# Layer 0's FFN: four constant products a block taken from VectorE, one to ScalarE and three to GpSimd

## The chip, the cores and the metric

The kernel runs on one core of a Trainium2 chip. The core has a matrix engine (TensorE, PE in the profile; its weight loads are PEld), a vector engine (VectorE, DVE), an activation engine (ScalarE, ACT), GpSimd (POOL) and SyncE (SP), which issues most transfers. Each engine works through its own queue in order and waits on semaphores for the others. The metric is the device time of one execution in microseconds. The matrix engine's clock can be throttled; the profile shows the granted share of full speed.

## What is computed

Two transformer layers over x of shape (2, 1024, 256), 2048 tokens in all. Each layer normalises x and adds an attention and an FFN of the same normalised input:

```python
x = L0_attn_x
xn = _layernorm(x, axis=-1)
x = x + _L0_attn_ref(xn, ...) + _L0_ffn_ref(xn, L0_ffn_w_gating, L0_ffn_w_linear)
xn = _layernorm(x, axis=-1)
x = x + _L1_attn_ref(xn, ...) + _L1_ffn_ref(xn, L1_ffn_w_gate_up, L1_ffn_w_proj)
```

The change lies in layer 0's FFN, with inputs rounded to an 8-bit float and results in bfloat16:

```python
def _qdot(x, w, out_dtype=BF16):
    return jnp.dot(x.astype(E4M3), w.astype(E4M3), preferred_element_type=out_dtype)
ff_gate = _qdot(x, w_gating[0])
gate_value = jax.nn.gelu(ff_gate)
ff1 = _qdot(x, w_gating[1])
activations = gate_value * ff1
outputs = _qdot(activations, w_linear)
```

gelu is the tanh form: with g the gate, 0.5 (1 + tanh(c0 (g + c1 g^3))) g, every step rounded to bfloat16. Layer 0's attention is causal, with 32 heads of 8 columns over 1024 keys, and takes an exact maximum of each row of scores before the exponentials. Layer 1's attention is over 16 heads for each token, its FFN has ternary weights.

## The kernel before

Layer 0 is one loop over slots in `attention0`. A slot is one call of `weigh` (L929): four matmuls give two score tiles of 128 keys x (4 heads x 128 queries) (L934), two exponentials on ScalarE turn them into p (L944), on the diagonal GpSimd clears what lies above it (L948), and one group later `gather` (L962) multiplies p with the values (L964). There are 288 such slots, for 16 blocks of 128 queries (`order`).

Between them, ahead by three query blocks, run the units of maxima (`max_unit`, L859): matmuls of scores into PSUM (L870, and L847 for the causal mask), and a reduction by VectorE over the keys (L882). Their tiles have three PSUM buffers. A finished block of maxima goes through L909 and L911, by DRAM, into rows of `qlast`, and its queries come by L799; the loop starts a query block only ten slots after its maxima (`LEAD`).

`one_slot` (L1134) paces three things into each slot: units of maxima by a credit, and one piece of layer 0's FFN at a time, so that 171 pieces spread over the slots. A piece is what lies between two `yield`s of `weights0` (L203, the rounding of the weights) or `ffn0` (L231). A piece is issued under `tc.issue_after(reduced.ins)`, that is, behind the last reduction given out so far. TensorE's order is that of the program text (`manual_schedule` for PE); for the other engines the framework's scheduler orders the queues.

`ffn0` works through four chunks of 512 tokens, and in each through four blocks `h2` of two hidden chunks: 16 blocks. A block makes gate and f1 for 2 x 128 hidden columns (L283), which ScalarE copies to bfloat16 tiles of 128 x 1024, `g` and `f1` (L286). Then come Square on ScalarE (L289) and the gelu chain on VectorE (L290 to L300) with Tanh on ScalarE in its middle (L295). The function `e4m3` (L182) rounds the product to the 8-bit grid in four steps (L190, L193, L195, L198) and a fifth, the check (L200), multiplies by a large constant and its inverse so that what overflows the format becomes infinite or not a number, as in the reference. The tiles `fs` (f1 and w1), `fg` (g), `fw` (w2) and `fe` have one buffer each, `act` has five. When a chunk's four `act` tiles are there and the next chunk's first block is through, `out_piece` (L240) makes the output matmuls (L243); ScalarE copies them (L252, L253) and GpSimd adds them to x (L256).

GpSimd also rounds layer 1's weights to ternary values, four steps for each of twelve pieces (L333 to L336) followed by a load (L321), and does part of preparing queries and keys (L711, L715, L750) and the residual adds of attention (L1007, L1008).

Of the kernel before, what the change touches and what calls it, by code (L numbers as in the profile page):

```python
# [11 lines left out]
BF = mybir.dt.bfloat16  # L12
I32 = mybir.dt.int32
U16 = mybir.dt.uint16
AF = mybir.ActivationFunctionType
ALU = mybir.AluOpType
# [28 lines left out]
E4_BIG = 1.109375 * 2.0**119  # L45
# [3 lines left out]
def two_layers(ctx: ExitStack, tc: tile.TileContext, a: dict, out: bass.AP):  # L49
    nc = tc.nc  # L50
# [128 lines left out]
                nc.scalar.copy(xnT[c][:, k, :], ps[k])  # L179
            yield  # L180

    def e4m3(dst, src, e, s, check):  # L182

        wide = src.dtype == F32
        as_int = I32 if wide else U16
        big = 1.5 * 2.0 ** (20 if wide else 4)
        nc.vector.tensor_scalar(  # L190
            e.bitcast(as_int), src.bitcast(as_int), 0x7F800000 if wide else 0x7F80, None, ALU.bitwise_and
        )
        nc.vector.tensor_scalar(e, e, E4_MIN, big, ALU.max, ALU.mult)  # L193
        yield
        nc.vector.tensor_tensor(s, src, e, ALU.add)  # L195
        if wide:
            yield
        nc.vector.tensor_tensor(dst, s, e, ALU.subtract)  # L198
        if check:
            nc.vector.tensor_scalar(dst, dst, E4_BIG, 1.0 / E4_BIG, ALU.mult, ALU.mult)  # L200


    def weights0(pool, scratch):  # L203

        wg = pool.tile([P, 2, 2, HID], BF, tag="wg", name="wg", bufs=1)
        wl = pool.tile([P, NHC, D], BF, tag="wl", name="wl", bufs=1)
        stage = scratch
        dst = [wg[:, g, k, :] for g in range(2) for k in range(2)]
        dst += [wl[:, 4 * h : 4 * h + 4, :].rearrange("p c d -> p (c d)") for h in range(2)]

        def load(n):
            st = stage[n % 4]
            if n < 4:

                (nc.sync if n < 1 else nc.gpsimd).dma_start(out=st, in_=a["w_gating"][n // 2, n % 2 * P : n % 2 * P + P, :])
            else:
                nc.gpsimd.dma_start(
                    out=st.rearrange("p (c d) -> p c d", d=D),
                    in_=a["w_linear"][(n - 4) * 512 : (n - 3) * 512, :].rearrange("(c p) d -> p c d", p=P),
                )  # L220

        load(0)
        yield wg, wl
        for n in range(6):
            e, s = (pool.tile([P, 1024], F32, tag=x, name=f"{x}w{n}", bufs=1) for x in ("fe", "fs"))
            yield from e4m3(dst[n], stage[n % 4], e, s, True)
            for m in range(1, 4) if n == 0 else [n + 3] if n < 3 else []:
                load(m)
            yield

    def ffn0(pool, psp, weights, add_done):  # L231

        wg, wl = weights
        acts = {}

        def e_tile(dt, name):
            t = pool.tile([P, 1024], F32, tag="fe", name=name, bufs=1)
            return t if dt == F32 else t.bitcast(BF)[:, 0:1024]

        def out_piece(n, i):  # L240
            po = psp.tile([P, D], F32, tag="t", name=f"f0o{n}_{i}")
            for hc in range(NHC):
                nc.tensor.matmul(  # L243
                    po,
                    acts[n][hc // 2][:, hc % 2 * 512 + i * P : hc % 2 * 512 + (i + 1) * P],
                    wl[:, hc, :],
                    start=(hc == 0),
                    stop=(hc == NHC - 1),
                )

            ob = pool.tile([P, 2, D], BF, tag="ob", name=f"ob{n}_{i}", bufs=1)
            nc.scalar.copy(ob[:, 0], po)  # L252
            nc.scalar.activation(ob[:, 1], po, AF.Copy, scale=0.0)  # L253
            x_i = xs[4 * n + i]
            for j in range(2):
                nc.gpsimd.tensor_tensor(x_i, x_i, ob[:, j], ALU.add)  # L256
            add_done(4 * n + i)

        order = (0, 1, 3, 2)
        for m, n in enumerate(order):  # L260
            wide = pool.tile([P, 1024], F32, tag="fs", name=f"fsx{n}", bufs=1)
            xq = pool.tile([P, 2, 512], BF, tag="xq", name=f"xq{n}", bufs=1)
            yield from e4m3(
                xq.rearrange("p k t -> p (k t)"),
                xnT[n].rearrange("p k t -> p (k t)"),
                e_tile(F32, f"fex{n}"),
                wide,
                False,
            )
            yield  # L270
            acts[n] = []
            for h2 in range(NHC // 2):
                nm = f"{n}_{h2}"
                wide = pool.tile([P, 1024], F32, tag="fs", name=f"fs{nm}", bufs=1)
                w1, f1 = (wide.bitcast(BF)[:, k * 1024 : (k + 1) * 1024] for k in range(2))
                g = pool.tile([P, 1024], BF, tag="fg", name=f"fg{nm}", bufs=1)
                w2 = pool.tile([P, 1024], BF, tag="fw", name=f"fw{nm}", bufs=1)
                for j in range(2):
                    hc = 2 * h2 + j
                    for u, to in enumerate((g, f1)):  # L280
                        ps = psp.tile([P, 512], F32, tag="t", name=f"gu{nm}_{j}{u}")
                        for k in range(2):
                            nc.tensor.matmul(  # L283
                                ps, wg[:, u, k, hc * P : (hc + 1) * P], xq[:, k, :], start=(k == 0), stop=(k == 1)
                            )
                        nc.scalar.copy(to[:, j * 512 : (j + 1) * 512], ps)  # L286
                    yield

                nc.scalar.activation(w1, g, AF.Square)  # L289
                nc.vector.tensor_mul(w1, w1, g)  # L290
                nc.vector.tensor_scalar(w1, w1, GELU_C1, None, ALU.mult)
                yield
                nc.vector.tensor_add(w1, g, w1)
                nc.vector.tensor_scalar(w1, w1, GELU_C0, None, ALU.mult)
                nc.scalar.activation(w2, w1, AF.Tanh)  # L295
                yield
                nc.vector.tensor_scalar(w2, w2, 1.0, 0.5, ALU.add, ALU.mult)
                nc.vector.tensor_mul(w2, g, w2)
                yield
                nc.vector.tensor_mul(w2, w2, f1)  # L300
                yield
                act = pool.tile([P, 1024], BF, tag="act", name=f"act{nm}", bufs=5)
                yield from e4m3(act, w2, e_tile(BF, f"fe{nm}"), w1, True)
                acts[n].append(act)
                yield
                if m and h2 == 0:
                    for i in range(4):
                        out_piece(order[m - 1], i)
                        yield
        for i in range(4):  # L310
            out_piece(order[-1], i)
            yield
# [365 lines left out]
    def attention0(w, qlast, tables):  # L678
# [11 lines left out]
        with ExitStack() as es:  # L690
# [418 lines left out]
            acc = ps_acc.tile([P, 512], F32, tag="acc", name="acc0")  # L1109
            nc.vector.memset(acc, 0.0)  # L1110
            pieces = itertools.chain(conversions, ffn0(pool, ps_t, weights, add_done))
            at = 0
            credit = share = 0.0
# [79 lines left out]
def _bf(v):  # L1193
    import ml_dtypes
    import numpy as np

    return float(np.float32(v).astype(ml_dtypes.bfloat16))
# [7 lines left out]
GELU_C0 = _bf((2.0 / PI) ** 0.5)  # L1205
GELU_C1 = _bf(0.044715)
# [77 lines left out]
```

## Time and profile before

| what | value |
|---|---|
| median of 3 runs | 1200.87 us (1200.59 to 1201.39) |
| the profiled execution's own time | 1200.35 us |
| its span, first to last instruction | 1198.6 us |
| TensorE busy in the span | 1016.8 us, 85% |
| VectorE busy | 745.6 us, 62% |
| ScalarE busy | 574.3 us, 48% |
| GpSimd busy | 335.7 us, 28% |
| mean granted clock | 0.913 |

The profile is one execution. Busy time counts the instructions of an engine; matmuls overlap and their ends are modelled. Layer 0 ends and layer 1 begins at about 780 us. The page's slices (40 equal parts of the span, tenths of busy time; a slice is 30 us) show where each engine is full:

```profile
PE   5463887897989989888989998978999999998884
DVE  6677988899688998698986888162323223323220
ACT  1112462672556757576767776731424414414421
POOL 2023233314243120412134246453312212312200
```

VectorE is nearly full up to slice 24 and a third full afterwards; TensorE is nearly full from slice 6 to the end. An idle gap on one engine is put down to what ended it: "idle before" names the instruction of another engine, or the transfer, that came last. The chain of waits goes back from the last instruction, at each step to what released it.

Rows of the VectorE chain of one block, as groups (busy us, mean ns, idle time before and what ended it):

```profile
L290 DVE TENSOR_TENSOR fs<-fs,fg 128x1024 bf16<-128x1024 bf16 x16 | 11.3, 705 | 0.0
L293 DVE TENSOR_TENSOR fs<-fg,fs 128x1024 bf16<-128x1024 bf16 x16 | 12.8, 799 | 0.0
L298 DVE TENSOR_TENSOR fw<-fg,fw 128x1024 bf16<-128x1024 bf16 x16 | 12.6, 788 | 0.3
L300 DVE TENSOR_TENSOR fw<-fw,fs 128x1024 bf16<-128x1024 bf16 x16 | 11.7, 732 | 0.0
```

### The profile page before, as it was taken

The page shows a single profiled execution, that of the slowest core. Times are in us where ns is not written, and L with a number is a line of the kernel's source. Part 1 is how long each engine was busy: PE and PEld are TensorE (multiplying, and loading weights), DVE is VectorE, ACT ScalarE, POOL GpSimd, SP SyncE. Part 2 cuts the span into 40 slices and gives each one's busy share as a digit, 9 for nine tenths or more (in the row PEclk, how much of TensorE's full clock was granted, in tenths as well). Part 3 has the DMA queues.
Part 4 walks back from the last instruction along what each step waited for, and adds up shares of the span by engine and source line. Part 5 has one row for each costly group of instructions (what it writes and reads, how often), then busy time and mean ns, then how long its engine had stood idle before and what let it go on. Part 6 is the DMA issues. An engine that isn't in the chain of part 4 may idle for free.

```text
span 1198.6 us, 18891 instructions
## 1 busy us (share of the span) xinstructions
PE 1016.8 (85%) x7228; PEld 487.4 (41%) x7228; DVE 745.6 (62%) x1416; ACT 574.3 (48%) x1006; POOL 335.7 (28%) x384
## 2 busy tenths in 40 slices
PE   5463887897989989888989998978999999998884
PEld 2231332232433222232323334234676676675663
DVE  6677988899688998698986888162323223323220
ACT  1112462672556757576767776731424414414421
POOL 2023233314243120412134246453312212312200
PEclk8676797997899989998989999999999999998985
DMA  6631001002101010101010110047111421421202
GB/s 191 157 98 37 22 5 46 11 20 60 34 17 36 3 25 19 36 1 27 2 27 3 25 27 5 2 55 114 37 28 45 76 41 42 80 41 29 45 11 53
DMA packets 79012, 48.99 MB, mean 41 GB/s; under 512 B 31721, under 2 KB 73705, under 8 KB 78921
## 3 DMA queue, kind: packets, MB, share of 16 engines
q1 hardware_dynamic: 75960, 43.58, 17.1%
q0 software_dynamic: 2960, 4.20, 1.7%
q8 instruction: 57, 0.93, 0.3%
q14 instruction: 35, 0.28, 0.1%
HBM read 33.59 MB, written 15.73 MB: 41 GB/s over the span
## 4 chain that ended last, share of the span: by engine, by line
PE 53%; DVE 25%; DMA 7%; ACT 6%; issue 4%; POOL 3%; SPq 2%; ACTq 0%; POOLq 0%; DVEq 0%
DVE mx L882 14%; PE acc L964 8%; PE f1gu L609 7%; PE s L934 7%; PE f1o L640 5%; PE m L870 4%; PE sk L519 3%; PE sq L484 3%; PE gu L283 2%; ACT p L527 2%; DMA qkv<-all 2%; PE m L847 2%; PE acc L534 2%; ACT p L944 1%; PE ao L585 1%
## 5 line engine op out<-in xcount | busy, mean ns | idle before, releaser
L882 DVE TENSOR_REDUCE mx<-m 128x1 f32<-128x512 f32 (+3 forms) x608 | 372.8, 655 | 90.0 <-PE m L870 52.1
L944 ACT ACTIVATE p<-s 128x512 f32<-128x512 f32 x576 | 306.8, 604 | 147.0 <-PE s L934 143.8
L964 PE MATMUL acc<-p,v 128*9 128x512 f32 x1152 | 172.4, 623 | 1.8 <-ACT p L944 1.2
L870 PE MATMUL m<-k,qmain 64*128 64x512 bf16 (+3 forms) x384 | 93.9, 363 | 52.9 <-DVE mx L882 36.0
L948 POOL TENSOR_SCALAR_AFFINE_SELECT p<-p 128x512 f32<-128x512 f32 x128 | 84.3, 682 | 177.2 <-ACT p L944 176.9
L609 PE MATMUL f1gu<-xnT,wgu 128*128 128x512 f32 x256 | 118.4, 606 | 1.6 <-DVE wgu L1189 1.6
L870 PE MATMUL m<-kmain,qmain 64*128 64x512 bf16 (+3 forms) x384 | 83.8, 333 | 24.3 <-DVE mx L882 22.1
L870 PEld LDWEIGHTS <-qmain 64*128 64x128 bf16 x768 | 50.2, 100 | 88.2 <-issue 63.0
L617 DVE TENSOR_TENSOR h<-f1gu,h 128x512 f32<-128x512 f32 x32 | 22.1, 692 | 99.6 <-PE f1gu L609 99.6
L621 POOL TENSOR_TENSOR sq<-h 128x512 f32<-128x512 f32 x28 | 29.1, 1039 | 189.5 <-DVE h L617 189.5
L847 PEld LDWEIGHTS <-ident_h 64*128 64x128 bf16 x832 | 45.1, 97 | 85.0 <-issue 62.2
L934 PE MATMUL s<-qlast,k 35*128 35x512 bf16 x288 | 65.4, 399 | 16.2 <-DMA qlast<-mscr 16.2
L847 PE MATMUL m<-mask_q,ident_h 64*128 64x128 bf16 (+3 forms) x832 | 75.0, 222 | 3.2 <-DVE mx L882 2.2
L934 PE MATMUL s<-qmain,k 64*128 64x512 bf16 x288 | 68.9, 400 | 8.8 <-DVE att L987 3.0
L609 PEld LDWEIGHTS f1gu<-xnT,wgu 128*128 128x128 f32 x256 | 47.8, 196 | 51.2 <-issue 48.4
L934 PE MATMUL s<-qmain,kmain 64*128 64x512 bf16 x288 | 64.1, 390 | 5.2 <-ACT p L944 2.6
L934 PEld LDWEIGHTS <-k 64*128 64x128 bf16 (+1 forms) x576 | 21.2, 96 | 114.5 <-issue 106.1
L492 DVE TENSOR_REDUCE m<-sq 128x16 f32<-128x2048 f32 x16 | 36.7, 2292 | 44.1 <-PE sq L484 42.6
L934 PE MATMUL s<-qlast,klast 35*128 35x512 bf16 x288 | 61.2, 386 | 0.0
L640 PE MATMUL f1o<-k,h 128*128 128x256 f32 x256 | 59.4, 389 | 0.0
L640 PEld LDWEIGHTS f1o<-k,h 128*128 128x128 f32 x256 | 49.4, 194 | 8.4 <-issue 1.1
L484 PE MATMUL sq<-ks,qs 24*128 24x128 f32 x512 | 34.7, 414 | 14.5 <-ACT p L527 13.7
(264 smaller groups left out, 1541.4 us busy)
## 6 DMA issues: line engine op xcount, KB each, us to landing
qmain<-qscr SPq DMA_DIRECT2D x64, 96.0 KB
qkv<-all SPq DMA_DIRECT2D x16, 384.0 KB
qscr<-ptq SPq DMA_DIRECT2D x32, 96.0 KB
x<-in_x SPq DMA_DIRECT2D x16, 128.0 KB
qmain<-qscr SPq DMA_DIRECT2D x32, 64.0 KB
qs<-qkv SPq DMA_DIRECT2D x16, 128.0 KB
ks<-qkv SPq DMA_DIRECT2D x16, 128.0 KB
vs<-qkv SPq DMA_DIRECT2D x16, 128.0 KB
```

The source lines that it names most:

```text
L484: nc.tensor.matmul(ps[:, s, r, :], columns(q, slice(S * s, S * s + HD + 8), 4 * b + r), columns(k, slice(S * s, S * s + HD + 8), 4 * b + r ...
L492: nc.vector.tensor_reduce(m, ps, AX.X, ALU.max, negate=True)
L519: nc.tensor.matmul(ps[:, s, r, :], columns(k, slice(S * s, S * s + HD + 9), 4 * b + r), columns(q, slice(S * s, S * s + HD + 9), 4 * b + r ...
L609: nc.tensor.matmul(ps[g], wgu[:, k, g * HID + hc * P : g * HID + (hc + 1) * P], xnT[n][:, k, :], start=(k == 0), stop=(k == 1),)
L640: nc.tensor.matmul(po, hs[hc // 2][:, hc % 2, i * P : (i + 1) * P], wp[:, hc, :], start=(hc == 0), stop=(hc == NHC - 1),)
L847: nc.tensor.matmul(out[e][:, :, lo:], ident_h[rows, t, :], rhs.to_broadcast([HALF, out[e].shape[1], P - lo]), start=start and t == 0, stop ...
L870: nc.tensor.matmul(sc[e][:, s * width : (s + 1) * width], qst[b, i][0][rows, p, :], kst[b][0][rows, p // 4, lo : lo + width], start=not fo ...
L882: reduced = nc.vector.tensor_reduce(mx[b, i][:, part, e, pairs[0] : pairs[0] + n], sc[e][:, : n * width].rearrange("p (s k) -> p s k", s=n ...
L934: nc.tensor.matmul(sc[e], kst[b][n][rows, u, j * P : (j + 1) * P], qst[b, i][n][rows, 4 * u : 4 * u + 4, :], start=n == 0, stop=n == 1,)
L944: nc.scalar.activation(p, sc[e], AF.Exp, scale=scale)
L948: nc.gpsimd.affine_select(out=by_head, in_=by_head, compare_op=ALU.is_ge, fill=0.0, base=0, pattern=[[0, 4], [1, P]], channel_multiplier=-1,)
L964: nc.tensor.matmul(acc[32 * s : 32 * s + HD0 + 1, :], vst[b][:, j, 4 * G + s, :], ps[s], start=(j == 0), stop=(j == i),)
```

## The change

In each of the 16 blocks of `ffn0` four products with constants leave VectorE. The product with c1 (L291), `(w2 + 1) * 0.5` (L297) and the check of `e4m3` (L200) go to GpSimd; the product with c0 (L294) becomes a Copy with a scale on ScalarE. The check of the weights in `weights0` stays on VectorE. The `yield` that stood between L298 and L300 now stands before L298, so the number of pieces is as before.

```diff
-    def e4m3(dst, src, e, s, check):
+    def e4m3(dst, src, e, s, check, checker=nc.vector):
...
         nc.vector.tensor_tensor(dst, s, e, ALU.subtract)
         if check:
-            nc.vector.tensor_scalar(dst, dst, E4_BIG, 1.0 / E4_BIG, ALU.mult, ALU.mult)
+            checker.tensor_scalar(dst, dst, E4_BIG, 1.0 / E4_BIG, ALU.mult, ALU.mult)
...
                 nc.scalar.activation(w1, g, AF.Square)
                 nc.vector.tensor_mul(w1, w1, g)
-                nc.vector.tensor_scalar(w1, w1, GELU_C1, None, ALU.mult)
+                nc.gpsimd.tensor_scalar(w1, w1, GELU_C1, None, ALU.mult)
                 yield
                 nc.vector.tensor_add(w1, g, w1)
-                nc.vector.tensor_scalar(w1, w1, GELU_C0, None, ALU.mult)
+                nc.scalar.activation(w1, w1, AF.Copy, scale=GELU_C0)
                 nc.scalar.activation(w2, w1, AF.Tanh)
                 yield
-                nc.vector.tensor_scalar(w2, w2, 1.0, 0.5, ALU.add, ALU.mult)
+                nc.gpsimd.tensor_scalar(w2, w2, 1.0, 0.5, ALU.add, ALU.mult)
+                yield
                 nc.vector.tensor_mul(w2, g, w2)
-                yield
                 nc.vector.tensor_mul(w2, w2, f1)
                 yield
                 act = pool.tile([P, 1024], BF, tag="act", name=f"act{nm}", bufs=5)
-                yield from e4m3(act, w2, e_tile(BF, f"fe{nm}"), w1, True)
+                yield from e4m3(act, w2, e_tile(BF, f"fe{nm}"), w1, True, nc.gpsimd)
```

All line numbers in this document are those of the kernel before. In the changed kernel the same lines stand one further down from L289 on, and L298 two.

## The prediction

> **What bounds the kernel now.** I read first the busy time by stage. Layer 0's FFN vector work (sixteen blocks of gelu, one per pair of hidden chunks) starts at 167 us and ends at 731 us, so the stage is 175 to 735 us. The columns are length, then busy time and count of TensorE, its weight loads, VectorE, ScalarE and GpSimd, the granted clock, DMA share and GB/s.
>
> ```profile
> 175.00:735.00 560.00, 492.99 (x3649) 166.17 (x3651) 478.27 (x904) 351.74 (x675) 171.86 (x201) 0.94 0.10 23
> 735.00:780.00 45.00, 42.03 (x287) 13.89 (x286) 15.29 (x37) 34.37 (x69) 25.38 (x37) 1.00 0.01 3
> ```
>
> TensorE and VectorE are both near full and neither is full: 67 us idle on the one, 82 on the other. Second, the table of who waited for whom in that stage (total us, times, longest):
>
> ```profile
> PE m L870 <- DVE mx L882: 43.0, 75, 2.8
> DVE mx L882 <- PE m L870: 43.7, 40, 3.2
> DVE mx L882 <- PE m L847: 24.8, 32, 3.3
> PE s L934 <- ACT p L944: 3.7, 10, 0.6
> ACT fw L295 <- DVE fs L294: 12.8, 9, 7.4
> ```
>
> The score tiles of the maxima (three PSUM buffers) couple the two: TensorE waits 43 us for reductions, VectorE 68.5 us for scores. They pass the lead to and fro. Third, the chain of waits: adding its pieces between 175 and 735 us by engine gives TensorE 266.0, VectorE 240.2, ScalarE 22.8, GpSimd 19.2, issue 11.6. So half of VectorE's busy time (240 of 478), 6.5% of ScalarE's (22.8 of 352) and 11% of GpSimd's (19.2 of 172) lie on it. I use these shares below for time that is added to an engine at a place I cannot name.
>
> **What is removed from VectorE.** Four instructions in each of 16 blocks; the last of these rows counts six weight checks of the same line apart:
>
> ```profile
> L291 DVE TENSOR_SCALAR fs<-fs x16: 375/418/1259, 168.5 to 708.6; 128x1024 bf16<-128x1024 bf16 x16
> L294 DVE TENSOR_SCALAR fs<-fs x16: 376/426/1261, 177.4 to 710.9; 128x1024 bf16<-128x1024 bf16 x16
> L297 DVE TENSOR_SCALAR fw<-fw x16: 410/427/904, 182.9 to 715.1; 128x1024 bf16<-128x1024 bf16 x16
> L200 DVE TENSOR_SCALAR act<-act x16: 410/420/853, 200.3 to 730.7; 128x1024 bf16<-128x1024 bf16 x16
> ```
>
> (minimum/median/maximum ns.) Their means are 522, 562, 503 and 471 ns: 16 x 2.058 = 32.9 us of busy time. But the next instruction starts before the recorded end: in the timeline L291 starts at 462.32 and its successor at 462.65, L294 at 466.65 and 466.99, L297 at 468.19 and 468.66, L200 at 480.30 and 480.63. In steps a block gives back 0.33 + 0.34 + 0.47 + 0.33 = 1.47 us, 23.5 us in all, and some 4 us more for the instances that were stretched. What of it lies on the path: the chain's pieces on these lines add up to 4.1 (L291) + 5.7 (L294) + 3.9 (L297) + 2.7 (L200) = 16.3 us. That is the bound of the gain. Since each engine holds the lead in turn, TensorE's own queue will take over in part of these places; its 43 us of waiting for reductions are 64% of its 67 idle us. I take 0.7 of 16.3, **-11.4 us**; bounds half (-8.2) and all (-16.3).
>
> **What is added to ScalarE.** 16 Copy activations of 128x1024, in the same queue just ahead of Tanh. Square and Tanh of that shape step in 0.96 us (458.91 to 459.86, 467.11 to 468.07): 15.4 us, times 6.5%, **+1.0 us**. Behind each stand exponentials (L944), for which TensorE waits little now (3.7 us in the waits above). No table load is added in the order of the changed queue.
>
> **What is added to GpSimd.** 48 one-input products of 128x1024 bf16. The trace has no such row. The nearest:
>
> ```profile
> masks.py:199 POOL TENSOR_SCALAR_AFFINE_SELECT ident<-ident 128x128 f32<-128x128 f32 x1 | 0.3, 287 | 0.0
> L948 POOL TENSOR_SCALAR_AFFINE_SELECT p<-p x128: 624/634/1172, 105.7 to 780.0; 128x512 f32<-128x512 f32 x128
> L335 POOL TENSOR_TENSOR tmg<-tmg,twg 128x512 bf16<-128x512 bf16 x8 | 9.6, 1198 | 0.5
> ```
>
> One-input selects grow by (634 - 287)/384 = 0.9 ns an element, so 634 + 512 x 0.9 = 1.1 us at 1024; two-input products at twice L335 would be 2.4 us. I take 1.1, since the new operation has one input; 2.4 stays as the upper end. 48 x 1.1 = 53 us on an engine that is 31% busy. By the 11% share that would be 5.9 us; but what stands behind the products are ternary weights for layer 1, residual adds, and the diagonal's selects, whose consumer (L964) comes a slot later, so I take a third, **+2.0 us** (bounds 0 and 5.9). L200 of the last block stands before the final output matmuls: L198 ends at 730.18 and L243 went on at 731.20; with GpSimd free at 729.64 it goes on at about 731.4, **+0.2 us**.
>
> **The waits that the change adds.** VectorE runs in order, so it now stops at L293 until GpSimd has done the product that was L291, and at L298 until ScalarE has done Copy and Tanh and GpSimd the product that was L297; behind it wait the reductions, and for these TensorE. I took the changed program's VectorE queue and added the steps (and present idle time) of what stands between. From L290 to L293 the cover of the 16 blocks is 7.1, 4.1, 1.2, 3.3, 0.9, 6.1, 1.2, 3.6, 3.4, 4.1, 3.8, 0.4, 2.4, 3.6, 4.1, 1.5 us. Needed: 1.1 + 0.1 for two handovers, plus GpSimd's backlog where its previous instruction ended after L290 (1.4, 1.5, 1.1 and 0.5 us in blocks 1, 5, 8, 9). Only blocks 5 and 12 fall short, by 1.8 and 0.8: 2.6 us; at 2.4 us a product it is 8.9. From L293 to L298 the cover is 7.5, 5.2, 4.2, 7.8, 5.0, 4.1, 6.0, 3.6, 4.8, 4.8, 7.4, 4.8, 5.5, 3.6, 6.4, 8.7 us. Needed: half an exponential in front (0.3), Copy 1.06, one exponential between (0.52; the changed ScalarE queue has one or another instruction there in 12 blocks), Tanh 1.06, the product 1.1, handovers 0.15: 4.2 us. Short by 1.4 us in all. Together 4.0 us of stall, half on the path: **+2.0 us**.
>
> **The shared memory port.** In the timeline around 655 us L882 starts at 654.85 while GpSimd runs L334 and keeps its 0.60 us step; L293 behind it starts as GpSimd starts L335, and takes 1.68 us instead of 0.68:
>
> ```profile
> 654.20 1.15 POOL L334 TENSOR_TENSOR tmp<-tmp,tsp 128x512 bf16<-128x512 bf16 x1
> 655.43 1.15 POOL L335 TENSOR_TENSOR tmp<-tmp,twp 128x512 bf16<-128x512 bf16 x1
> 654.85 0.68 DVE L882 TENSOR_REDUCE mx<-m 128x1 f32<-128x512 f32 x1
> 655.45 1.68 DVE L293 TENSOR_TENSOR fs<-fg,fs 128x1024 bf16<-128x1024 bf16 x1
> ```
>
> The first one or two instructions beside the 48 new products are reductions out of PSUM in about 40 places, other work in about 8; 8 x half a product (0.55) = 4.4 us, a third on the path since much of that is not followed by a reduction, **+1.5 us** (bounds 0, and 8 x 1.0 = 8).
>
> The Trainium skill's page "SBUF — State Buffer", section "Who interferes with whom", speaks against the change: a GpSimd instruction and a VectorE instruction with two SBUF inputs, or in a two-port mode, exclude each other for the whole instruction, while reductions never contend. The rows above agree on both kinds. If every one of the 48 products held up a VectorE instruction for the 1.0 us seen, half on the path, the sum would turn to +18 us; by the rows, with reductions beside most, it stays below zero.
>
> **Sum.** -11.4 + 1.0 + 2.0 + 0.2 + 2.0 + 1.5 = -4.7 us. TensorE's queue is the same instruction for instruction; in SyncE's queue two of 515 transfers move up: one store of L783, issued at 183.68, to just behind its two sisters at 178.67, past L909, L911 and ten loads of L799, and one load of L799 past two L911 near 418 us. What they pass is issued one step later (0.31 to 0.44 us between issues there), which I cost at nothing: the rows that L911 brings are used at least ten slots of some 2 us later; without that lead it would be 0.8 us. From 780 us on, layer 1 is untouched. The profiled execution took 1200.35 us (span 1198.6 and 1.75 around it), so 1195.7 by it; the median of the runs is 1200.87, 0.5 above. I predict **1196.2 us**.
>
> **Rivals.**
> (1) The whole chain part comes free and the covers hold: -16.3 + 1.0 + 0.5 = -14.8, 1186 us. For it: most covers exceed the need. Against: VectorE's own 68.5 us of waiting for TensorE. 0.14.
> (2) Nothing measurable: TensorE takes over at once, half of 16.3 comes free and the costs of 6.7 eat it: -1.5, 1199.4 us. For it: TensorE holds the larger part of the chain. 0.20 for an end within 0.2% of the time before (2.4 us, about what a measurement of this kernel can tell from no change).
> (3) The round trip becomes VectorE's new stop at L298. If the exponential between Copy and Tanh waits for its scores (L944 waits for L934 116.6 us in 104 times now, 1.1 each) and a product takes 2.4 us, the need is 6.6 us, the shortfall at L298 21.3 us, at L293 8.9. Half of 30.2 is 15.1: -11.4 + 15.1 + 6.0 for the rest of the costs, with GpSimd's queue 1.3 dearer, gives +9.7, 1210.6 us. It breaks even at 13 us of stall and is told from no change at 18. For it: four covers lie within 0.2 us of 4.2 or below it. Against: three of four terms must go to their bad end. 0.24.
> (4) VectorE isn't relieved, since the products hold the port against its remaining two-input work: 48 holds as above. Against: the order, with reductions beside them. 0.04.
>
> **How the numbers follow.** The forecast (1189 to 1198) has 0.38. Faster: 0.38 + 0.14 = 0.52; same 0.20; slower 0.24 + 0.04 = 0.28. The range reaches from (1) to (3), 1186 to 1210.
>
> **What would show it.** Right: VectorE busy about 30 us lower in the stage, the product rows on GpSimd near 1.1 us, idle time before L293 and L298 a few us in all, TensorE's 43 us of waiting for L882 some 5 to 10 lower. Wrong: idle time before L298 above 13 us with ScalarE's Tanh or GpSimd's product named as its end, product rows near 2.4 us, or L290 to L198 stretched past the medians above; and if VectorE's idle time for TensorE grows by all that was taken off, rival (2).

## The result, and the profile after

| | before | changed |
|---|---|---|
| median | 1201.13 us (4 runs, 1200.59 to 1203.3) | 1219.15 us (4 runs, 1212.83 to 1221.48) |
| ratio | | 1.0135, 95% interval 1.0109 to 1.016 |
| profiled execution, span | 1200.35, 1198.6 us | 1220.01, 1218.3 us |

The change makes the kernel 1.35% slower. Layer 0 pays nearly all of it: layer 1's first FFN matmul (L609) starts at 791.9 us before and at 809.8 us in the changed kernel, 17.9 of the 19.7 us between the spans.

Line numbers in the views of the changed kernel are one higher from L289 on (L883 is the reduction L882, L292 the c1 product, L294 the addition behind it). Its stages, with the columns of the prediction's first view; the FFN blocks now end near 750 us:

```profile
175.00:740.00 565.00, 491.07 (x3518) 161.66 (x3533) 444.45 (x813) 360.10 (x677) 240.72 (x240) 0.93 0.09 22
740.00:800.00 60.00, 55.24 (x411) 19.26 (x405) 26.00 (x64) 41.48 (x83) 33.66 (x47) 0.97 0.01 3
```

VectorE's busy time falls as worked out (478 to 444 us, in stages of 560 and 565 us), GpSimd's rises by 79 us over the span (335.7 to 415.0) where 53 were expected, and the stage needs more time. VectorE's waits for scores from 167 to 755 us before:

```profile
DVE mx L882 <- PE m L870: 45.3, 41, 3.2
DVE mx L882 <- PE m L847: 24.8, 32, 3.3
```

The waits in the same stretch of the changed kernel:

```profile
PE m L871 <- DVE mx L883: 44.1, 72, 3.0
PE acc L965 <- ACT p L945: 6.6, 5, 4.2
...
DVE mx L883 <- PE m L871: 50.8, 45, 3.7
DVE mx L883 <- PE m L848: 44.6, 39, 3.3
DVE fs L294 <- POOL fs L292: 14.1, 7, 3.8
...
ACT fs L295 <- DVE fs L294: 18.7, 9, 6.7
```

TensorE waits as long for reductions as before (43.0 then) although VectorE has 34 us less to do. VectorE waits 25 us more for scores (95.4 after 70.1), and there is one new line: it stops 14.1 us, in seven places, for the c1 product on GpSimd. None stands for L298 (here L300). The rows of the three products on GpSimd and of the Copy on ScalarE (minimum/median/maximum ns) tell why:

```profile
L292 POOL TENSOR_SCALAR fs<-fs x16: 2760/2768/3146, 169.9 to 724.4; 128x1024 bf16<-128x1024 bf16 x16
L298 POOL TENSOR_SCALAR fw<-fw x16: 1038/1043/1056, 180.5 to 730.5; 128x1024 bf16<-128x1024 bf16 x16
L200 POOL TENSOR_SCALAR act<-act x16: 1034/1043/2025, 198.5 to 747.1; 128x1024 bf16<-128x1024 bf16 x16
L295 ACT ACTIVATE fs<-fs x16: 1047/1056/1089, 178.1 to 727.9; 128x1024 bf16<-128x1024 bf16 x16
```

Three products of one shape and type on one engine: two take 1.04 us, the third 2.77. One such stop in the timeline of the changed kernel, first VectorE, then GpSimd, then TensorE (start, length, instruction, idle time before it and what ended it):

```profile
573.12 0.68 DVE L291 TENSOR_TENSOR fs<-fs,fg 128x1024 bf16<-128x1024 bf16 x1
573.72 0.25 DVE L984 RECIPROCAL z<-ot 128x16 f32<-128x16 f32 x1
574.01 0.29 DVE L988 TENSOR_TENSOR att<-ot,z 128x128 f32<-128x128 f32 x1
576.70 0.69 DVE L294 TENSOR_TENSOR fs<-fg,fs 128x1024 bf16<-128x1024 bf16 x1 [2.40 <-POOL fs L292]
577.31 2.48 DVE L883 TENSOR_REDUCE mx<-m 128x1 f32<-128x512 f32 x4
...
573.89 2.77 POOL L292 TENSOR_SCALAR fs<-fs 128x1024 bf16<-128x1024 bf16 x1 [5.88 <-DVE fs L291]
...
578.05 0.37 PE L871 MATMUL m<-kmain,qmain 64*128 64x512 bf16 x1 [2.02 <-DVE mx L883]
```

Between L291 and L294 the queue holds only two short instructions of the attention. VectorE stands still 2.40 us, and four reductions that need neither tile stand behind it; TensorE, which waits for a score buffer, stands still 2.02 us. The chain of waits agrees, by engine (shares of the span):

```profile
PE 53%; DVE 21%; ACT 7%; POOL 7%; DMA 6%; issue 5%; SPq 1%; ACTq 0%; POOLq 0%; DVEq 0%
```

VectorE had 25%, GpSimd 3% and ScalarE 6%. Adding the pieces from 167 to 755 us, VectorE's part is 192 us (244 before), GpSimd's 66.5 (19.2 before), of which the c1 product alone has 25.0, and ScalarE's 42.9 (27.7 before).

### The profile page after: what moved, and what is told of

Its sections match the earlier page's. It is cut to its first block, busy times and chain, and to the rows that moved or that the text cites. A ratio compares the mean times of both kernels' runs of the same rounds, so it can differ in the third digit from the quotient of the medians.

```text
span 1218.3 us, 18798 instructions
## 1 busy us (share of the span) xinstructions
PE 1025.9 (84%) x7212; PEld 487.7 (40%) x7228; DVE 722.4 (59%) x1352; ACT 589.3 (48%) x1022; POOL 415.0 (34%) x432
## 4 chain that ended last, share of the span: by engine, by line
PE 53%; DVE 21%; ACT 7%; POOL 7%; DMA 6%; issue 5%; SPq 1%; ACTq 0%; POOLq 0%; DVEq 0%
DVE mx L883 11%; PE acc L965 9%; PE f1gu L610 8%; PE s L935 7%; PE f1o L641 5%; PE m L871 3%; PE sk L520 3%; PE sq L485 3%; POOL fs L292 2%; PE gu L283 2%; ACT p L945 2%; ACT p L528 2%; PE m L848 2%; PE acc L535 2%; PE ao L586 1%
## 5 line engine op out<-in xcount | busy, mean ns | idle before, releaser
L883 DVE TENSOR_REDUCE mx<-m 128x1 f32<-128x512 f32 (+3 forms) x608 | 371.3, 654 | 118.5 <-PE m L871 61.4
L965 PE MATMUL acc<-p,v 128*9 128x512 f32 x1152 | 185.3, 630 | 7.8 <-ACT p L945 6.6
L292 POOL TENSOR_SCALAR fs<-fs 128x1024 bf16<-128x1024 bf16 x16 | 44.8, 2800 | 59.5 <-DVE fs L291 59.0
```

The lines of the kernel that those rows point to most:

```text
L292: nc.gpsimd.tensor_scalar(w1, w1, GELU_C1, None, ALU.mult)
L883: reduced = nc.vector.tensor_reduce(mx[b, i][:, part, e, pairs[0] : pairs[0] + n], sc[e][:, : n * width].rearrange("p (s k) -> p s k", s=n ...
L965: nc.tensor.matmul(acc[32 * s : 32 * s + HD0 + 1, :], vst[b][:, j, 4 * G + s, :], ps[s], start=(j == 0), stop=(j == i),)
```

## The experiments

Theory A: the c1 product, 2.77 us on GpSimd, makes the loss. Theory B: the longer round trip before L298 and the fuller queues make it. Ratios are to the kernel before, run on the same chip.

| kernel | median us | ratio, 95% interval |
|---|---|---|
| changed kernel | 1219.15 | 1.0135 (1.0109 to 1.016) |
| c1 product back on VectorE | 1202.07 | 0.9994 (0.9979 to 1.0009) |
| c1 product as two operations | 1204.38 | 1.0008 (0.9994 to 1.0023) |
| c1 move alone | 1218.51 | 1.0125 (1.0106 to 1.0145) |
| four products left out | 1187.14 | 0.9869 (0.985 to 0.9888) |
| check move alone | 1199.94 | 0.9969 (0.9955 to 0.9983) |
| c0 move alone | 1202.62 | 0.9992 (0.9976 to 1.0009) |
| halving move alone | 1194.66 | 0.9928 (0.991 to 0.9946) |
| c1 as two operations, and check | 1202.63 | 0.9998 (0.9979 to 1.0018) |
| halving and check | 1198.76 | 0.9973 (0.9955 to 0.9991) |
| yield alone | 1201.42 | 0.9992 (0.9975 to 1.0008) |
| c1 as two operations, halving, check | 1201.35 | 0.9987 (0.9963 to 1.0011) |
| four left out, Copy put in | 1196.57 | 0.9943 (0.9924 to 0.9963) |

**The c1 product.** Three kernels: put back, written with a second operation, and moved alone.

```diff
-                nc.gpsimd.tensor_scalar(w1, w1, GELU_C1, None, ALU.mult)
+                nc.vector.tensor_scalar(w1, w1, GELU_C1, None, ALU.mult)
```

> The changed kernel with the product with c1 put back on VectorE; the other three products stay moved. Theory A (the c1 product takes 2.77 us on GpSimd where its two sisters take 1.04, VectorE stops at L293 for it, and this alone makes the loss): 1194 to 1202 us, idle time before L293 gone. Theory B (the round trip through ScalarE and GpSimd before L298, and GpSimd's and ScalarE's fuller queues, make the loss): 1210 us or more, as only one of the four moves is undone.

```diff
-                nc.gpsimd.tensor_scalar(w1, w1, GELU_C1, None, ALU.mult)
+                nc.gpsimd.tensor_scalar(w1, w1, GELU_C1, 1.0, ALU.mult, ALU.mult)
```

> The changed kernel with the c1 product on GpSimd written as two products, with c1 and with 1.0, which gives the same numbers. Theory A with the form as the cause of the 2.77 us: the product takes 1.04 us like its two-operation sisters, and the time is 1194 to 1204 us. Theory A with another cause of the 2.77 us (operands, place): 2.77 us again and 1217 to 1221 us. Theory B: 1.04 us or not, still 1210 us or more.

The third is the kernel before with L291 alone on GpSimd, in its one-operation form.

> The kernel before with the c1 product alone moved to GpSimd. Theory A: most of the loss with a quarter of the change, 1211 to 1222 us, and idle time before L293 of 14 us or more. Theory B: 1199 to 1205 us, since there is no longer way to L298 and GpSimd's queue gains 16 instructions instead of 48.

0.9994, 1.0008 and 1.0125: theory A on all three, though the medians of the first two lie 0.1 and 0.4 us above its ranges; theory B's are 8 and 6 us away from them. In the second, the same product on the same tile at the same place, with a factor of 1.0 behind it, takes 1.04 us instead of 2.77, and VectorE's stop falls from 14.1 to 4.1 us, as the view of this one line says:

```profile
L292 POOL TENSOR_SCALAR fs<-fs x16: 1033/1043/1414, 170.2 to 712.8; 128x1024 bf16<-128x1024 bf16 x16
...
who waited for it (us, times):
  DVE fs L294: 4.1, 3
```

So the cause of the 2.77 us is the form of the instruction, one operation in place of two; what GpSimd does differently with the two forms no run here shows. Another order of the queues is not behind it: in the traces of these two kernels the instructions of VectorE, of ScalarE and of GpSimd stand in the same order. From 1.0135 to 1.0008 the form costs 15 us; the c1 move alone, with all else as before, costs as much (1.0125 x 1203.3 is 15.0 us above it), with the same stop, in the same view of that kernel:

```profile
L291 POOL TENSOR_SCALAR fs<-fs x16: 2759/2767/3142, 168.0 to 723.2; 128x1024 bf16<-128x1024 bf16 x16
...
who waited for it (us, times):
  DVE fs L293: 14.1, 7
```

The Trainium skill's page "GPSIMD Engine Reference", section "Engine selection", says of one-input operations on GpSimd that they run at roughly line rate. The two-operation form agrees, taking as long (1.04 us for 1024 elements in each partition) as ScalarE's Copy of that shape (1.06); the one-operation form does not, with 2.77 us, and the measurement decides.

**The relief by itself.** The kernel before without the four products: both factors in the tanh argument, the halving and the check.

```diff
-                nc.vector.tensor_scalar(w1, w1, GELU_C1, None, ALU.mult)
...
-                nc.vector.tensor_scalar(w1, w1, GELU_C0, None, ALU.mult)
...
-                nc.vector.tensor_scalar(w2, w2, 1.0, 0.5, ALU.add, ALU.mult)
...
-                yield from e4m3(act, w2, e_tile(BF, f"fe{nm}"), w1, True)
+                yield from e4m3(act, w2, e_tile(BF, f"fe{nm}"), w1, False)
```

> The kernel before with the four products left out of layer 0's FFN blocks (c1, c0, the halving and the check), so its output differs; nothing is put on another engine. It prices the relief of VectorE by itself. If the prediction's term is right: 11.4 us less, about 1190 (bounds 1185 and 1193). If TensorE takes over at once: 1198 to 1201.

0.9869, or (1 - 0.9869) x 1203.3 = 15.8 us less (13.5 to 18.1): not the 11.4 of the prediction, but close to the chain's whole 16.3. TensorE did not take back a third of the relief: its waiting for reductions falls from 43.0 to 35.2 us in the table of waits (L867 and L879 are L870 and L882 here), though its part of the chain grows (from 284.6 to 306.7 us between 167 and 755 us).

```profile
PE m L867 <- DVE mx L879: 35.2, 69, 4.2
```

With the two-operation form the changed kernel is still no faster than before (1.0008). About 16.7 us (0.9869 to 1.0008) are what the four moves themselves cost. The next kernels ask which.

**One move at a time.** The check alone (only the last argument and the engine of L200):

> The kernel before with the check of the FFN's blocks alone moved to GpSimd (1.04 us each there, and no VectorE instruction waits for it). A move that adds no wait should give its share of the relief of 15.7 us that leaving all four out gave: by the chain's pieces 2.7 of 16.3, so 2 to 4 us less (ratio 0.997 to 0.998). If GpSimd's queue or the shared port takes it back: 0.999 or more.

0.9969, 3.7 us less, as expected of a move that nothing on VectorE waits for.

The c0 product alone:

```diff
-                nc.vector.tensor_scalar(w1, w1, GELU_C0, None, ALU.mult)
+                nc.scalar.activation(w1, w1, AF.Copy, scale=GELU_C0)
```

> The kernel before with the c0 product alone moved to ScalarE, as a Copy ahead of Tanh. Theory S (the Copy, 0.96 us on ScalarE with exponentials behind it, gives back its relief and more): same or slower, ratio 1.000 to 1.004. Theory G (GpSimd's halving product before L298 is what gives the relief back): 0.993 to 0.997, as its part of the relief is 5.7 of 16.3 by the chain's pieces.

The halving alone:

```diff
-                nc.vector.tensor_scalar(w2, w2, 1.0, 0.5, ALU.add, ALU.mult)
+                nc.gpsimd.tensor_scalar(w2, w2, 1.0, 0.5, ALU.add, ALU.mult)
+                yield
                 nc.vector.tensor_mul(w2, g, w2)
-                yield
```

> The kernel before with the halving product alone moved to GpSimd, with the changed place of the yield (L298 and L300 in one piece). Theory S: 0.996 to 0.998 (its part of the relief is 3.9 of 16.3, and 1.04 us more before L298 is mostly covered). Theory G: 1.000 to 1.006, with VectorE idle before L298 or its reductions late.

The c0 move gives nothing that can be measured (0.9992, just under theory S's range), the halving 8.7 us (0.9928): theory S in kind, though that lies below both ranges and the halving gains twice what its chain share said. The other place of the yield is not why:

> The kernel before with the yield moved from behind L298 to in front of it and nothing else, so VectorE has the same instructions. If the halving's gain comes from the relief: 0.999 to 1.001 here. If it comes from the other grouping of the pieces: 0.993 to 0.996.

0.9992, no change by the place of the yield. The order of the queue is not why either: in the traces of these two kernels VectorE's instructions stand in the same order but for the halving and four others. So the halving on GpSimd itself gives the gain. Its instruction was the one on VectorE that waited for Tanh (0.2 us before), but why the gain exceeds the 3.9 us of its pieces stays open.

Two observations bear on that. The gain is not spread over the blocks: the addition L293 of the fifth block starts at 318.2 us (325.8 before, 322.9 with the yield alone), that of the last at 702.5 (710.2 and 707.5), so all of it is there after five of 16 blocks. And the granted clock was 0.914 to 0.920 in its six runs, 0.903 to 0.913 in the 29 of the kernel before beside them. Among these 29, 0.001 more went with 0.56 us less, so the 0.0076 between the means would go with some 4 of the 8.7 us, as an estimate. The yield alone had 0.910 to 0.917 and was not measurably faster, and no run tells whether the clock is a cause of the shorter time or goes with it.

The trace of the c0 move alone shows where it costs, in VectorE's waits:

```profile
DVE fw L297 <- ACT fw L295: 6.5, 7, 1.5
```

With the Copy ahead of it, Tanh ends later, and VectorE stops at L297 seven times.

**The Copy with the relief held.** The kernel without the four products, with one line more:

```diff
+                nc.scalar.activation(w1, w1, AF.Copy, scale=GELU_C0)
                 nc.scalar.activation(w2, w1, AF.Tanh)
```

> The kernel without the four products (0.9869 before), with a Copy of 128x1024 with the factor c0 put ahead of Tanh on ScalarE, so the output differs from the reference in the other three products only. It prices the Copy alone, with VectorE's relief held. The prediction's term was 1.0 us (6.5% of 15.4): 0.9875 to 0.9885. Theory S: 4 us or more, 0.990 to 0.995, and more ScalarE on the chain of waits.

0.9943 against 0.9869: 0.0074 x 1202.5 = 8.9 us for the Copy (5.6 to 12.2 by the two intervals; the two were run on different chips), where the prediction had 1.0. The view of waits has the larger part of it, the stop at L297 (L296 here):

```profile
DVE fw L296 <- ACT fw L294: 6.4, 6, 1.5
```

ScalarE's part of the chain grows from 37.7 to 55.7 us between the two kernels, with 8.9 for the Copy itself, 5.6 more for Tanh and 4.8 more for the exponentials behind (and 1.3 less elsewhere).

**Pairs and triples.** The c1 product as two operations with the check; the halving with the check; and the changed kernel with two-operation c1 and with c0 back on VectorE:

> The kernel before with the c1 product (in the two-operation form) and the check on GpSimd, and the c0 and halving products left on VectorE, so the way from L293 to L298 is as before. If the round trip through ScalarE and GpSimd before L298 is what gives the relief back (S and G together): 0.994 to 0.998, faster than the kernel before. If GpSimd's load as such does: 0.999 to 1.003.

> The kernel before with the halving product and the check on GpSimd; c1 and c0 stay on VectorE (the changed kernel without its two moves in the first half of the chain). If the single results add up (0.9969 for the check, 0.9928 for the halving): 0.988 to 0.991, the fastest version so far. If GpSimd's load makes the two get in each other's way: 0.993 to 0.997. Against the changed kernel without the c1 move (0.9994) it also prices the Copy on ScalarE in that company: a gap of about 0.01 would be 12 us.

> The changed kernel with the c1 product in the two-operation form and the c0 product back on VectorE: three products on GpSimd, none on ScalarE. Theory S (the Copy on ScalarE gives back what it relieves and more): clearly faster than the same with the Copy (1.0008), 0.991 to 0.996. If the c1 move, even at 1.06 us, costs what it relieves: no better than with the c1 product on VectorE, 0.990 to 0.994, so between them. If the Copy is innocent: 1.000 to 1.003.

0.9998, 0.9973 and 0.9987. The first lands where GpSimd's load as such was named. That is not shown to be the cause, since the stop of 4.1 us at L293 is in its waits again: against the check alone (0.9969) the c1 move costs about 3.5 us net even at 1.04 us, with intervals that overlap slightly. The second falls a little above its second range and says that gains do not add up: halving and check together gain less (0.9973) than the halving alone (0.9928, on another chip), though VectorE waits for neither. The third falls between its ranges; its interval, from 0.9963 to 1.0011, lies just above both of the faster ones, so putting c0 back is not the clear gain that theory S forecast. Against the second, the changed kernel with c1 back (0.9994, the same with the c0 product as a Copy) is 0.2% slower, and against the third the two-operation kernel (1.0008) is as much slower, 2.5 us each time, with intervals that overlap. That fits the Copy's 8.9 us less the 5.7 us of c0's pieces on VectorE. Why halving and check get in each other's way stays open; VectorE's order in the halving with the check differs from that in the halving alone, the checks apart, in four instructions only. The fastest version that computes the same is the halving move alone: 1194.66 us, 0.9928 (0.991 to 0.9946), faster than both kernels of the case.

## Why the prediction was wrong, by its steps

- **Sign and range.** 1196.2 us (1186 to 1210), faster, was forecast; 1219.15 was measured, outside the range.
- **The step that failed: the price of a product on GpSimd ("I take 1.1, since the new operation has one input; 2.4 stays as the upper end").** 1.1 us was right for two of the three products (1.04) and wrong for the third, which lay above the upper end too (2.77). I priced three instructions by one row because each has one input and one shape; they differ in the form, and the trace of before had no row of a product with a constant on GpSimd at all.
- **The covers were right, one backlog was not.** Put into the same table, 2.77 + 0.1 us and GpSimd's backlog leave blocks 3, 5, 7, 8, 12, 13 and 16 short, by 1.7 + 3.5 + 1.7 + 0.4 + 2.5 + 0.5 + 1.4 = 11.7 us; the profile shows stops in these seven blocks, of 1.7, 3.1, 1.7, 0.3, 2.4, 3.8 and 1.1 us, 14.1 in all. At 1.1 us it had two stops, in blocks 5 and 12, and 2.6 us; with the two-operation form blocks 5, 12 and 13 stop, by 4.1 us. Block 13 is where the table errs, and the trace of before shows why: I gave it no backlog, but GpSimd's ternary rounding and the load behind it held its queue for 3.4 us after L290's end, and with them the block is 3.8 us short.

```profile
604.86 1.06 DVE L290 TENSOR_TENSOR fs<-fs,fg 128x1024 bf16<-128x1024 bf16 x1
...
607.00 1.21 POOL L336 TENSOR_TENSOR wgu_bf<-tmg,twg 128x512 bf16<-128x512 bf16 x1
608.51 0.77 POOL L321 DMA_DIRECT2D twp<-in_w_proj  x1 [0.30 <-POOL wgu_bf L336]
```

- **"Half on the path" was too little.** The stop grew by 10 us (4.1 to 14.1) and the time by 15. A stop of VectorE puts all reductions behind it late, and TensorE's wait comes after VectorE's own, as in the timeline at 573 us; the share of busy time on the chain says nothing of that.
- **Relief of VectorE, -11.4:** 15.8 measured; right in kind, too small. The factor 0.7, for TensorE taking over, does not show in the result.
- **Copy on ScalarE, +1.0:** 8.9 measured with the relief held. I priced it as busy time by ScalarE's share of the chain; but it stands between two VectorE instructions, so its length is a wait, and where Tanh's consumer is on VectorE, as in that run, it stopped it by 6.4 us.
- **The stop at L298, +2.0 with that at L293:** no such stop in the changed kernel. The need of 4.2 us was covered.
- **The port, +1.5:** L298 and L300 did get longer, from means of 788 and 732 to 834 and 870 ns, that is 16 x 0.184 = 2.9 us; L190 and L193 got shorter by 69 and 28 ns, 1.6 us, and L293 by 58 ns, 0.9 us. A small term in busy time; its part on the path was not measured.
- **The sum without the failed step.** Even with 1.04 us for all three the change is no gain: 1.0008, against 0.9961 by my sum. The Copy's 7.9 us too few and the relief's 4.4 too few bring that sum of -4.7 to -1.2, or 0.999; the rest is within the intervals. That is no proof of these terms, since the gains of single moves do not add up here.
- **Rivals.** (3) had the kind of loss, a stop of VectorE for another engine, and its break-even of 13 us of stall, but put most of it, 21.3 of 30.2 us, at L298. (2) and (4) are refused by the 15.8 us of relief and by the lengths above. (1)'s 16.3 was nearly right for the relief, and its 0.5 us for the stops and GpSimd's queue was not.
- **Signs to look for.** VectorE's busy time fell as said, and TensorE's wait for reductions did not; of the signs of a wrong forecast, a product row of 2.4 us or more was there (2.77), and idle time above 13 us (14.1), before L293 and not before L298.

## What to carry to other kernels

Price each moved instruction in its own form: operation count, not only shape and type; an unseen form on an engine is an unknown, and its upper end is not bounded by a neighbour's row. Work that is moved out of a dependent chain and back into an in-order queue is paid as latency: count what lies between producer and consumer, and weigh a shortfall at more than half its length where another engine waits in turn: here 10 us of stops cost 15. Move first what nothing waits for, or the one product whose consumer has cover, and measure each move alone: here one of four moves by itself gave 8.7 us, and the four together lost 18.

## What was not expected of the hardware

A one-operation product on GpSimd took 2.77 us and the same with a second factor 1.04, on 128x1024 bfloat16, with nothing else different in the kernel.

The granted clock and the time went together between the runs of one program: of the changed kernel's four runs three have a granted clock of 0.906 to 0.907 and 1218.3 to 1221.5 us, the fourth 0.915 and 1212.83 us.
